# Decoder layer with a delta-rule scan, attention and experts: inverting by blocks of 32 rows and two rounds of doubling

## The chip, the cores and the metric

The kernel runs on one core of a Trainium2 chip. The metric is the device time of one execution in microseconds; a comparison of two kernels goes by the medians of their runs. The profile is one execution, recorded by the hardware.

## The reference

The input `x` is 32 sequences of 112 tokens with 256 features. One layer adds three blocks to it, each behind a layer norm: a recurrent block (an exponential average of the values, a delta-rule scan, a gated MLP), an attention with 16 heads over 375 context tokens, and a mixture of six experts of which each token takes two, with one shared expert. What the change touches is the scan:

```python
def step(S, inp):
    q_t, k_t, v_t, b_t = inp
    Sk = jnp.einsum('bij,bj->bi', S, k_t)
    S = S + b_t[:, None, None] * (v_t - Sk)[:, :, None] * k_t[:, None, :]
    o_t = jnp.einsum('bij,bj->bi', S, q_t)
    return (S, o_t)
```

Over 112 steps this is a triangular system. With G the products of the keys of one sequence, scaled by beta and the keys' norms, the kernel inverts a unit lower triangular matrix of 112 by 112 for each sequence and multiplies the values by the inverse.

## The kernel before

The 32 sequences go in eight groups of four (`GB`). For each group the stream `delta_block` followed by `queries` (together `ahead(g)`) does the recurrent block and the queries of the attention. The attention of a group takes 16 steps, each four heads of one sequence: `scores` (products, then the mask and the row extreme on VectorE, the exponential on ScalarE), two steps later `turned` (transposes, copied back by ScalarE) and `product`. Keys and values of the next sequence come from `keys_values`. While the attention of group g runs, the recurrent block of group g + 1 runs beside it, with the experts' routing and the shared expert of group g - 1 (`mixture_sparse`). In the last group the tables of the tokens for each expert are built (`tables`), and after it the experts run over them (`sparse_tiles`).

The order is made when the program is built. All instructions go to a `Recorder`. Streams are generators; each `yield` ends a piece, and the loop at the end of the kernel takes pieces in turn, by the matmul time that group 0's pieces cost (a piece with almost none counts 1.4 us). `Recorder.flush` then plans all engines with a price for each instruction (`price`) and emits them by planned start: whoever is ready first, and among the ready ones the earliest recorded. The order of TensorE, VectorE and ScalarE is taken as it is planned (`manual_schedule`); GpSimd and SyncE are ordered by the framework from the order in which it gets them. Every engine runs its instructions in order, so an instruction that comes later than its price said holds up what was planned behind its readers. The price of an operation on GpSimd with n elements per partition, a line of `price`, is

```python
return 0.97 if "dma" in op else 0.1 + n / 430
```

`hold()` makes the last recorded instruction follow the last recorded one of TensorE in the plan; it adds no wait on the chip.

The inversion in `delta_block`: the matrix W goes to a table in memory (`blocks<-W`), so that its diagonal blocks of 16 rows can be read back with one block on each partition (L, `C<-blocks`). A forward substitution inverts all 28 blocks at once, 15 steps of two operations, a product `part` and a subtraction. It runs on VectorE in group 0 and on GpSimd in the others (`plain`). The inverse and its transpose go back to two tables, which were cleared when the kernel began, and come back as block diagonal matrices X and Y of all four sequences (`X<-blocks`, `Y<-blocks`). Then rounds of doubling join neighbouring blocks, from 16 to 32, 64 and 112 rows: C (G between the halves, made on GpSimd) times X, scaled to W, then Y times W, subtracted from X (the last round updates Y instead). From the second round on Y is X turned by TensorE. All names in the profile are those of the buffers: the substitution appears as `W<-C,W` and `W<-W` with 28 partitions, a round as `X,C`, `W,Y` and `ident,X`. Most lines of the profile are L381, where the recorder emits.

In the routing, `dispatch` casts the places of the tokens in the experts' lists to integers (`row_i`) and scatters the tokens' numbers there with eight indirect DMAs of GpSimd, two for each sequence (the first and the second expert).

Of the kernel before, what the change touches and what calls it, by code (L numbers as in the profile page):

```python
# [8 lines left out]
F32 = mybir.dt.float32  # L9
# [3 lines left out]
ALU = mybir.AluOpType  # L13
# [3 lines left out]
P = 128  # L17
GB = 4
BS = 16
NEG = -1.0e9  # L20
# [365 lines left out]
def tile_decoder(ctx: ExitStack, tc: tile.TileContext, t: dict, out: bass.AP):  # L386
# [5 lines left out]
    nc = tc.nc  # L392
# [42 lines left out]

    NB = GB * T // BS
    FAR = BS * T + BS
    blocks = [dram.tile([NB, FAR], F32, name=f"blocks_{i}") for i in range(3)]
    kept = [dram.tile([GB, T, D], F32, name=f"kept_{g}") for g in range(groups - 1)]
# [12 lines left out]
    levels = []  # L452
    s = BS
    while s < T:
# [29 lines left out]
    nothing = moe.at("hT", 0, [P, t["fc3T"].shape[0] // P, NT])  # L484
    nothing = nothing[:T].rearrange("p c n -> p (c n)")[:, : NB * FAR // T]
    nc.vector.memset(nothing, 0.0)

    unit = const.tile([NB, BS, BS], F32, tag="unit", name="unit")
    nc.gpsimd.memset(unit, 0.0)
    nc.gpsimd.affine_select(  # L490
        out=unit, in_=unit, pattern=[[1, BS], [-1, BS]], compare_op=ALU.not_equal, fill=1.0, base=0,
        channel_multiplier=0,
    )
    number = const.tile([T, 2, SB], F32, tag="number", name="number")
# [21 lines left out]
    for vx in vxs:  # L516
        nc.gpsimd.memset(vx[:, :, :, 1, :], 0.0)
    for table in blocks[1:]:
        nc.gpsimd.dma_start(
            out=table.rearrange("n f -> (n f)").rearrange("(p q) -> p q", p=T), in_=nothing  # L520
        )
    for table in lists:
# [73 lines left out]
    keys_first, mask_first = load_keys(0), load_mask(0)  # L596
    xwk, xwv = weight("xwkT"), weight("xwvT")
    n2 = per_feature("norm2_w")
    wo = weight("Wo")
    w_gate, w_up, w_down = weight("w_gate"), weight("w_up"), weight("w_down")  # L600
    xwq, xwo = weight("xwqT"), weight("xwoT")
    keys_second, mask_second = load_keys(1), load_mask(1)
    x_second = load_x(1)
    gb = const.tile([T, NE], F32, tag="gb", name="gb")
# [94 lines left out]
    def delta_block(g, xt):  # L699
# [81 lines left out]
        plain.tensor_tensor(W, G, bcast(br2, T), ALU.mult)  # L781
        low, inv, turned_inv = blocks
# [3 lines left out]
        diagonal = lambda m: m[:, : BS * T].rearrange("n (i t) -> n i t", t=T)[:, :, :BS]  # L786
        nc.sync.dma_start(out=square(low), in_=W)
        L = dlt.tile([NB, BS, BS], F32, tag="C", name=f"L_{g}", bufs=2)
        nc.sync.dma_start(out=L, in_=diagonal(low))
        yield  # L790
        R = dlt.tile([NB, BS * BS + (BS // 2) ** 2], F32, tag="W", name=f"R_{g}", bufs=2)
        inverse = R[:, : BS * BS].rearrange("p (i j) -> p i j", j=BS)
        plain.tensor_copy(inverse, unit)
        for j in range(BS - 1):
            shape = [NB, BS - 1 - j, j + 1]
            part = R[:, BS * BS : BS * BS + shape[1] * shape[2]].rearrange("p (i j) -> p i j", j=j + 1)
            to = inverse[:, j + 1 :, : j + 1]
            plain.tensor_tensor(
                part, L[:, j + 1 :, j : j + 1].to_broadcast(shape),
                inverse[:, j : j + 1, : j + 1].to_broadcast(shape), ALU.mult,  # L800
            )
            plain.tensor_tensor(to, to, part, ALU.subtract)
            if j in (4, 9):
                yield
# [5 lines left out]
        nc.sync.dma_start(out=X, in_=square(inv))  # L810
        nc.sync.dma_start(out=Y, in_=square(turned_inv))
        yield
        yield
# [7 lines left out]

        C = between_halves(0)
        for i in range(len(levels)):
            pw = bank("pw")
# [3 lines left out]
            nc.vector.tensor_tensor(W, pw[:T, :NT].rearrange("p (b t) -> p b t", b=GB), bcast(br2, T), ALU.mult)  # L828
            if i > 0:
                py = bank("py")  # L830
                for b in range(GB):
                    transpose(py[:T, b * T : (b + 1) * T], X[:, b, :], ident[:T, :T])
                Y = dlt.tile([T, GB, T], F32, tag="Y", name=f"Y_{g}_{i}")
                nc.scalar.copy(Y.rearrange("p b t -> p (b t)"), py[:T, :NT])
# [269 lines left out]
    def dispatch(g, a3, place, ge):  # L1104
# [332 lines left out]
    def drain(stream):  # L1437
        for _ in stream:
            pass
# [196 lines left out]
```

## Time and profile before

| | |
|---|---|
| median of 13 runs | 1426.28 us (1423.45 to 1433.17) |
| profiled execution | 1423.26 us |
| its span, first to last instruction | 1421.6 us |
| granted TensorE clock, mean | 0.981 |
| busy TensorE, VectorE, ScalarE, GpSimd | 1362.6, 954.0, 702.6, 318.9 us |
| substitution of one group on GpSimd | 30 instructions, 409.07 to 419.52 us in group 3 |
| first matmul of a round in group 3 | 423.86 us |

Busy time is the union of an engine's instructions. The slices of the page are a fortieth of the span each, 35.5 us. PE is TensorE, DVE is VectorE, ACT is ScalarE, POOL is GpSimd, SP is SyncE, whose queue issues nearly all loads. A wait is put down to the engine or DMA that came last. A matmul of 32-bit floats has two records in the trace, a transpose one.

### The profile page before, as it was taken

What the parts mean: (1) busy time and instruction counts of PE and PEld (TensorE: products, weight loads), DVE (VectorE), ACT (ScalarE), POOL (GpSimd) and SP (SyncE); (2) the same over time, 40 slices, a digit from 0 to 9 for tenths busy, and PEclk for the clock granted to TensorE, in tenths of its full rate; (3) what the DMA queues carried; (4) which work ended last, traced back from release to release, by engine and by line L of the source; (5) the groups of instructions that cost most, each with busy time, mean ns of one, the idle gap of its engine ahead of it and who ended that gap; (6) DMA issues with size and microseconds to landing.
All of it is one profiled execution on the core that took longest, in us unless ns stands there. A gap on an engine that the chain in (4) does not pass through costs nothing.

```text
span 1421.6 us, 26678 instructions
## 1 busy us (share of the span) xinstructions
PE 1362.6 (96%) x9716; PEld 926.1 (65%) x9716; DVE 954.0 (67%) x3164; ACT 702.6 (49%) x1946; POOL 318.9 (22%) x492
## 2 busy tenths in 40 slices
PE   6679999999999899999999999999999999999998
PEld 4456766676677566766676667666766676666665
DVE  6646666775787487758775877587756875455577
ACT  2112856654665366456655664566556673222110
POOL 3122000311041103120312031203120045566400
PEclk9779999999999999999999999999999999999999
DMA  7100100101010100110011001100115122222283
GB/s 226 38 8 13 35 17 17 46 20 42 17 49 18 34 26 19 47 32 27 19 47 41 18 20 46 40 19 20 46 30 163 30 44 75 87 87 86 68 237 104
DMA packets 77170, 73.13 MB, mean 51 GB/s; under 512 B 29864, under 2 KB 72808, under 8 KB 77040
## 3 DMA queue, kind: packets, MB, share of 16 engines
q1 hardware_dynamic: 69296, 56.00, 14.5%
q0 software_dynamic: 7744, 15.43, 3.7%
q8 instruction: 77, 1.26, 0.4%
q14 instruction: 53, 0.43, 0.1%
HBM read 51.12 MB, written 20.28 MB: 50 GB/s over the span
## 4 chain that ended last, share of the span: by engine, by line
PE 71%; DVE 9%; ACT 6%; POOL 4%; DMA 4%; issue 2%; another core or an unknown queue 1%; SPq 0%; DVEq 0%; ACTq 0%
PE bank L381 61%; PE bank L1335 7%; PE bank L1352 3%; POOL W L381 3%; ACT e L381 3%; ACT eT L381 2%; DMA blocks<-W 2%; DMA X<-blocks 1%; DVE e L381 1%; DVE x L381 1%; DVE W L381 1%; DVE rs_u L381 1%; DVE rs_i L381 1%; ACT h L381 1%; DMA C<-blocks 1%
## 5 line engine op out<-in xcount | busy, mean ns | idle before, releaser
L381 ACT ACTIVATE e<-e,nmx 112x375 f32<-112x375 f32 x512 | 306.4, 603 | 176.0 <-DVE nmx L381 175.7
L381 DVE CUSTOM_DVE_ANT_0 e<-bank,neg,flip 112x375 f32<-112x375 f32 x512 | 282.7, 603 | 36.6 <-PE bank L381 30.9
L381 ACT COPY eT<-bank 125x448 f32<-125x448 f32 x384 | 185.3, 530 | 91.1 <-PE bank L381 81.7
L381 PEld LDWEIGHTS bank<-ident,e 112*125 112x125 f32 x1536 | 185.7, 188 | 31.3 <-issue 9.9
L381 PE MATMUL bank<-ident,e 112*125 112x112 f32 x1536 | 201.4, 276 | 1.0 <-ACT e L381 0.7
L381 PE MATMUL bank<-kx,qz 32*112 32x375 f32 x1024 | 123.4, 521 | 0.0
L381 PEld LDWEIGHTS bank<-eT,vx 125*32 125x32 f32 x3072 | 69.2, 109 | 57.2 <-issue 40.5
L381 PE MATMUL bank<-eT,vx 125*32 125x112 f32 x3072 | 100.7, 263 | 5.1 <-ACT eT L381 5.1
L381 PE MATMUL bank<-w_xwvT,cT 128*125 128x256 f32 x384 | 102.7, 394 | 0.0
L1335 PE MATMUL bank<-ew,xT 128*128 x216 | 101.9, 595 | 0.4 <-DVE nmx L381 0.4
L381 DVE SCALAR_TENSOR_TENSOR hs<-hs,bank 128x256 f32<-128x256 f32 x108 | 45.4, 421 | 79.5 <-ACT hs L381 77.6
L381 ACT ACTIVATION_READ_ACCUMULATOR e<-e,nmx 112x1 f32 x512 | 98.1, 192 | 0.0
L381 PE MATMUL bank<-cT,w_xwkT 128*128 128x375 f32 x256 | 95.4, 498 | 2.5 <-ACT eT L381 2.5
L381 POOL TENSOR_TENSOR u<-h,nwb 112x1024 f32<-112x1024 f32 x7 | 16.9, 2416 | 296.4 <-issue 282.8
L381 ACT ACTIVATE hs<-bank 128x256 f32<-128x256 f32 x54 | 20.7, 384 | 118.0 <-PE bank L1335 112.4
L381 POOL DMA_INDIRECT lists<-number,row_i x56 | 52.7, 941 | 110.5 <-DVE tn L381 57.0
L381 PEld LDWEIGHTS bank<-w_xwvT,cT 128*125 128x125 f32 x384 | 67.9, 190 | 13.7 <-issue 5.7
L381 DVE SCALAR_TENSOR_TENSOR qk<-qk,bank 128x448 f32<-128x448 f32 x56 | 34.8, 621 | 62.6 <-ACT qk L381 55.3
L381 PEld LDWEIGHTS bank<-cT,w_xwkT 128*128 128x128 f32 x256 | 44.0, 190 | 38.2 <-issue 6.9
L381 PEld LDWEIGHTS bank<-kx,qz 32*112 32x112 f32 x1024 | 42.2, 170 | 39.9 <-issue 15.6
L381 POOL DMA_INDIRECT xg<-rows,take x54 | 52.4, 969 | 51.6 <-PE bank L381 48.5
L1363 POOL DMA_INDIRECT results<-y,put x54 | 53.1, 983 | 38.5 <-DVE y L381 33.6
(251 smaller groups left out, 2380.0 us busy)
## 6 DMA issues: line engine op xcount, KB each, us to landing
cT<-in_ctxT_dram SPq DMA_DIRECT2D x32, 375.0 KB
mk<-in_mask_dram SPq DMA_DIRECT2D x32, 164.1 KB
x<-in_x_dram SPq DMA_DIRECT2D x7, 448.0 KB
rows<-h SPq DMA_DIRECT2D x7, 448.0 KB
kept<-x SPq DMA_DIRECT2D x7, 448.0 KB
e<-results SPq DMA_DIRECT2D x6, 448.0 KB
eT<-results SPq DMA_DIRECT2D x4, 448.0 KB
out_dram<-x SPq DMA_DIRECT2D x4, 448.0 KB
```

The source lines that it names most:

```text
L381: getattr(getattr(self.nc, name), op)(*[real(a) for a in args], **{k: real(v) for k, v in kwargs.items()})
L1335: rec.nc.tensor.matmul(p.real(), xT[:, c, :], w13[:, bass.ds(at[i] * (NC * 2 * MI) + c * 2 * MI, 2 * MI)], start=(c == 0), stop=(c == NC - 1),
L1352: rec.nc.tensor.matmul(p[:, :D].real(), hT[:, c, :], w2[:, bass.ds(at[i] * (CH * D) + c * D, D)], start=(c == 0), stop=(c == CH - 1),)
L1363: sent = rec.nc.gpsimd.indirect_dma_start(out=results[:], out_offset=bass.IndirectOffsetOnAxis(ap=put[:, i : i + 1], axis=0), in_=y, in_of ...
```

## The change

Group 0 keeps blocks of 16 rows and three rounds. In the other groups the blocks have 32 rows (four for each sequence, the last reaching past row 112 into cleared memory), so 16 partitions hold all blocks, the substitution has 31 steps with up to 256 elements, and two rounds follow. There are three more tables for it, cleared by SyncE during group 0. The unit matrix is set by two memsets in place of a copy; L, the inverse and `part` lie in other buffers in these groups. The substitution yields four times in place of twice, and two pauses stand in these groups where group 0 has its first round; the places of the keys' pieces in group 0 are moved to match. The places are cast for each sequence by itself, held behind TensorE, and the scatters of a sequence follow their cast. The loads of the second sequence's keys and mask and of the second group's tokens come before seven weights.

```diff
-BS = 16
+SIZES = 16, 32
...
+    many = [GB * ((T + size - 1) // size) for size in SIZES]
+    blocks = [
+        [dram.tile([n, size * T + size], F32, name=f"blocks_{size}_{i}") for i in range(3)]
+        for n, size in zip(many, SIZES)
+    ]
...
+    keys_second, mask_second = load_keys(1), load_mask(1)
+    x_second = load_x(1)
     n2 = per_feature("norm2_w")
     wo = weight("Wo")
     w_gate, w_up, w_down = weight("w_gate"), weight("w_up"), weight("w_down")
     xwq, xwo = weight("xwqT"), weight("xwoT")
-    keys_second, mask_second = load_keys(1), load_mask(1)
-    x_second = load_x(1)
...
-        L = dlt.tile([NB, BS, BS], F32, tag="C", name=f"L_{g}", bufs=2)
+        if g == 0:
+            L = dlt.tile([n, size, size], F32, tag="C", name=f"L_{g}", bufs=2)
+            spare = dlt.tile([n, size * size + (size // 2) ** 2], F32, tag="W", name=f"R_{g}", bufs=2)
+            flat, spare = spare[:, : size * size], spare[:, size * size :]
+        else:
+
+            L = qk.rearrange("p c n -> p (c n)")[:n, : size * size].rearrange("p (i j) -> p i j", j=size)
+            flat = dlt.tile([n, size * size], F32, tag="u", name=f"R_{g}")
+            spare = dlt.tile([n, (size // 2) ** 2], F32, tag="vs", name=f"part_{g}")
         nc.sync.dma_start(out=L, in_=diagonal(low))
         yield
-        plain.tensor_copy(inverse, unit)
-        for j in range(BS - 1):
+        plain.memset(flat, 0.0)
+        plain.memset(flat[:, :: size + 1], 1.0)
+        for j in range(size - 1):
...
-            if j in (4, 9):
+            if (j + 1) % (size // 4) == size // 8:
                 yield
...
+        first = min(g, 1)
+        for _ in range(2 * first):
+            yield
         yield
         yield
...
-        C = between_halves(0)
-        for i in range(len(levels)):
+        C = between_halves(first)
+        for i in range(first, len(levels)):
...
-            if i > 0:
+            if i > first:
                 py = bank("py")
...
-        nc.vector.tensor_copy(row_i[:, :, two], row_f[:, :, two])
         for b in range(GB):
+            i = g * GB + b
+            nc.vector.tensor_copy(row_i[:, :, i : i + 1], row_f[:, :, i : i + 1])
+            rec.hold()
             for c in range(2):
-                i = g * GB + b
                 nc.gpsimd.indirect_dma_start(
...
-                rec.hold()
...
-        for _ in range({5: 2, 6: 2, 7: 2, 8: 2, 9: 1, 11: 1, 18: 2}.get(i, 0)):
+        for _ in range({5: 2, 6: 2, 7: 1, 8: 1, 9: 1, 10: 1, 11: 1, 13: 1, 20: 2}.get(i, 0)):
             next(early_kv, None)
...
+        if i == 12:
+            for table in blocks[1]:
+                cleared(table, nc.sync)
+                rec.hold()
```

More of the change, by code (lines that the diff above doesn't have):

```diff
@@ L434, in tile_decoder @@
     results = dram.tile([2 * SB * T + NTM * TM, D], F32, name="results")
-    NB = GB * T // BS
-    FAR = BS * T + BS
-    blocks = [dram.tile([NB, FAR], F32, name=f"blocks_{i}") for i in range(3)]
+    many = [GB * ((T + size - 1) // size) for size in SIZES]
[3 more added lines that the diff above has]
+    ]
     kept = [dram.tile([GB, T, D], F32, name=f"kept_{g}") for g in range(groups - 1)]
@@ L452, in tile_decoder @@
     levels = []
-    s = BS
+    s = SIZES[0]
     while s < T:
@@ L484, in tile_decoder, with cleared @@
     nothing = moe.at("hT", 0, [P, t["fc3T"].shape[0] // P, NT])
-    nothing = nothing[:T].rearrange("p c n -> p (c n)")[:, : NB * FAR // T]
+    nothing = nothing.rearrange("p c n -> p (c n)")
     nc.vector.memset(nothing, 0.0)
[L488 to L493, printed above, removed]
+    def cleared(table, queue):
+        n = table.shape[0] * table.shape[1]
+        p = next(p for p in range(P, 0, -1) if n % p == 0 and n // p <= nothing.shape[1])
+        flat = table.rearrange("n f -> (n f)").rearrange("(p q) -> p q", p=p)
+        queue.dma_start(out=flat, in_=nothing[:p, : n // p])
     number = const.tile([T, 2, SB], F32, tag="number", name="number")
@@ L517, in tile_decoder @@
         nc.gpsimd.memset(vx[:, :, :, 1, :], 0.0)
[L518 to L521, printed above, removed]
+    for table in blocks[0][1:]:
+        cleared(table, nc.gpsimd)
     for table in lists:
@@ L781, in delta_block @@
         plain.tensor_tensor(W, G, bcast(br2, T), ALU.mult)
-        low, inv, turned_inv = blocks
+        size, n = SIZES[min(g, 1)], many[min(g, 1)]
+        low, inv, turned_inv = blocks[min(g, 1)]
         square = lambda m: m.rearrange("(b k) f -> b (k f)", b=GB)[:, : T * T].rearrange(
@@ L785, in delta_block @@
         )
-        diagonal = lambda m: m[:, : BS * T].rearrange("n (i t) -> n i t", t=T)[:, :, :BS]
+        diagonal = lambda m: m[:, : size * T].rearrange("n (i t) -> n i t", t=T)[:, :, :size]
         nc.sync.dma_start(out=square(low), in_=W)
-        L = dlt.tile([NB, BS, BS], F32, tag="C", name=f"L_{g}", bufs=2)
+        if g == 0:
[6 more added lines that the diff above has]
+            spare = dlt.tile([n, (size // 2) ** 2], F32, tag="vs", name=f"part_{g}")
         nc.sync.dma_start(out=L, in_=diagonal(low))
         yield
-        R = dlt.tile([NB, BS * BS + (BS // 2) ** 2], F32, tag="W", name=f"R_{g}", bufs=2)
-        inverse = R[:, : BS * BS].rearrange("p (i j) -> p i j", j=BS)
-        plain.tensor_copy(inverse, unit)
-        for j in range(BS - 1):
-            shape = [NB, BS - 1 - j, j + 1]
-            part = R[:, BS * BS : BS * BS + shape[1] * shape[2]].rearrange("p (i j) -> p i j", j=j + 1)
+        inverse = flat.rearrange("p (i j) -> p i j", j=size)
+        plain.memset(flat, 0.0)
+        plain.memset(flat[:, :: size + 1], 1.0)
+        for j in range(size - 1):
+            shape = [n, size - 1 - j, j + 1]
+            part = spare[:, : shape[1] * shape[2]].rearrange("p (i j) -> p i j", j=j + 1)
             to = inverse[:, j + 1 :, : j + 1]
```

## The prediction

> **What bounds the kernel now.** I read the busy shares and slices of the page first, then stretches of one group, the waits, and the rows of TensorE and GpSimd around one substitution.
>
> ```profile
> PE 1362.6 (96%) x9716; PEld 926.1 (65%) x9716; DVE 954.0 (67%) x3164; ACT 702.6 (49%) x1946; POOL 318.9 (22%) x492
> ...
> PE   6679999999999899999999999999999999999998
> ```
>
> TensorE is full from slice 4 on; only the head (the first 140 us) has gaps. The stretches (columns: stretch, its length, busy of PE, weight loads, DVE, ACT, POOL, granted clock, DMA share):
>
> ```profile
> 57.50:80.00 22.50, 12.85 (x57) 11.15 (x58) 8.10 (x19) 1.70 (x3) 2.64 (x3) 0.54 0.10 20
> 121.00:135.00 14.00, 11.38 (x70) 8.82 (x71) 9.62 (x29) 1.70 (x3) 1.13 (x1) 0.88 0.01 1
> 404.00:424.00 20.00, 19.59 (x207) 13.91 (x206) 18.65 (x74) 16.94 (x51) 10.70 (x33) 1.00 0.23 56
> 598.00:740.00 142.00, 140.19 (x1118) 97.32 (x1117) 101.08 (x349) 82.89 (x232) 26.75 (x47) 1.00 0.12 31
> ```
>
> A steady group takes 142 us, 140.19 of them TensorE. So work taken from TensorE there is time, and so is any wait put on it. Its waits between 380 and 450 us:
>
> ```profile
> PE bank L381 <- DVE nT L381: 0.8, 1, 0.8
> PE bank L381 <- DMA X<-blocks: 0.4, 1, 0.4
> ```
>
> The second is the end of the substitution's trip through memory. The trip on GpSimd, then the rounds of doubling on TensorE:
>
> ```profile
> 403.84 0.93 POOL L381 TENSOR_TENSOR W<-G,br 112x448 f32<-112x448 f32 x1
> 409.07 0.21 POOL L381 TENSOR_TENSOR W<-C,W 28x15 f32<-28x15 f32 x1 [4.30 <-DMA C<-blocks]
> 409.36 0.22 POOL L381 TENSOR_TENSOR W<-W 28x15 f32<-28x15 f32 x1
> ...
> 413.85 0.30 POOL L381 TENSOR_TENSOR W<-C,W 28x64 f32<-28x64 f32 x1
> 414.22 0.31 POOL L381 TENSOR_TENSOR W<-W 28x64 f32<-28x64 f32 x1
> 414.61 0.30 POOL L381 TENSOR_TENSOR W<-C,W 28x63 f32<-28x63 f32 x1
> ...
> 419.31 0.21 POOL L381 TENSOR_TENSOR W<-W 28x15 f32<-28x15 f32 x1
> ```
>
> ```profile
> 423.86 1.01 PE L381 MATMUL bank<-X,C 112*112 112x112 f32 x8 [0.41 <-DMA X<-blocks]
> 424.71 1.65 PE L381 MATMUL bank<-w_gate_wT,nT 128*112 128x6 f32 x16
> 426.21 1.02 PE L381 MATMUL bank<-W,Y 112*112 112x112 f32 x8
> 427.07 1.03 PE L381 MATMUL bank<-w_xwoT,oTx 128*112 128x256 f32 x4
> ...
> 429.58 0.55 PE L381 MATMUL bank<-ident,X 112*112 112x112 f32 x4
> 429.97 1.04 PE L381 MATMUL bank<-ident,vo 128*112 128x128 f32 x8
> ```
>
> The order on TensorE is fixed when the program is built. X came 0.41 us after TensorE turned to it: the order puts other work over the trip, by its prices.
>
> **The round that goes.** One round is eight records X,C, eight W,Y and four turns of X. From start to next start they hold TensorE 424.71-423.86 = 0.85, 427.07-426.21 = 0.86 and 429.97-429.58 = 0.39: 2.1 us. Groups 2 to 7 run this in full stretches: 6 x 2.1 = 12.6 us less. Group 1 stands under the head.
>
> **The longer substitution.** A block of 16 takes 15 pairs of instructions and 2 x 680 elements per partition; one of 32 takes 31 pairs and 2 x 5,456. Start to start is 0.29 us at 15 elements and 0.38 (mean of 0.37 and 0.39) at 64: 0.262 us each and 1.84 ns an element. That gives 30 x 0.262 + 1,360 x 0.00184 = 10.4 us for now (measured 419.52-409.07 = 10.45) and 62 x 0.262 + 10,912 x 0.00184 = 36.3 us after. Up to 256 elements are not in the trace; the rows of 448 bound them: W (932 ns) gives 1.63 ns beyond 64, hence 34.0 us, C (1134 ns) 2.16 ns, hence 39.8. I keep 36.3, the slope of the same instruction.
>
> GpSimd has the room (26.75 of 142 us busy). What counts is when X comes against the order's price, 0.1 + n/430 a piece: 6.2 us now and 6.2 + 25.4 = 31.6 after. The overrun is 10.45-6.2 = 4.3 now, with a wait of 0.4, and 36.3-31.6 = 4.7 after. The wait grows by 0.4 us a group, 2.4 in six; at 34.0 it vanishes (-2.4), at 39.8 it grows by 3.9, or 23.
>
> "GPSIMD Engine Reference", Engine selection and the accounting before it, speaks against this change: elementwise work belongs on VectorE, and a two-input operation costs GpSimd 4497 ns at 2048 elements. As an estimate from that page, 2.2 ns an element makes 40.2 us and the sum below some 23 us worse. The rows up to 64 elements say 1.84 ns, and the sum stays on them.
>
> **What covers it.** X comes 25.9 us later after W. TensorE must live that long on attention, keys and values. In 404 to 424 it did, idle only for X; but DVE was busy 18.65 of 20 us and ACT 16.94. Part of DVE's load there is a layer norm that comes once a group. I take 0.5 us of new idleness a group, 3 in six; ends 0 and a tenth of the stretch, 2.6, or 16. The same later X leaves fewer microseconds for the rest of the chain; before, xwq of this group ran at 522, 98 us after X, so 72 remain for work that group 0, alone, did in 63 (second round at 67.9, xwq at 131.2), and I charge nothing; without that cover it is the second rival.
>
> The copy that turns the inverse grows from 256 to 1,024 elements (0.60 to at most 2.4 us), so Y comes 1.8 us later against X. Y had 1.6 us to spare (issued 0.7 behind X, read 2.35 behind). The order prices the copy at 2.5 and plans around it: nothing, at worst 0.2 a group.
>
> On SP the stores of the inverse wait 26 us longer; behind them stood `rows<-h` and a mask load. The order is worked out anew and puts loads that are ready ahead of them: nothing, or, if a keys load lands behind, the second rival. The two memsets (1,024 elements, about 2.4 us by the u row) fall into GpSimd's 19.8 idle us before C.
>
> **The head.** Group 0 substitutes on VectorE as before. Its read of L was issued at 38.69 us and such a read takes 1.8 (407.25 to 409.07), yet VectorE began at 50.44: group 1's norm stood before it, and x of group 1 kept that waiting till 37.7. Its load moves from issue 20.2 to about 11. I take 4 us earlier (0 to 9.9). Against it: between 121.1 and 131.2 TensorE filled a gap with 4.8 us of group 1's rounds. They now come after a substitution 26 us longer; 2.1 are gone, 2.7 move into full stretches. The gap also lowers the clock (8 records took 1.81 us at 0.54, 0.85 at 1.00): 1 us, 0 to 3. Sum -4 + 2.7 + 1 = -0.3; ends -7.2 and +5.7.
>
> "TensorE: Matmul & The Clock Gate", Part 1, puts the fall of the clock after about 3.4 us without work. By it the waits for X above cost no clock; the 0.54 above is the case of this trace.
>
> **The rest.** Weights that now load later (Wo read at 86.9, w_gate at 100.7) have over 50 us. Clearing three tables by SP near 70 us falls where DMA is 0.10 busy; without that cover 3 x 226 KB at the 226 GB/s of the first slice cost 3 us. Three more casts a group, at 0.17 us, lie on VectorE at 67%. The eight scatters ran in one row (458.7 to 468.3), whatever the order said; now each pair waits for its cast. On GpSimd the gathers of the lists queue behind. In the last group scatters ended at 1144.5 and TensorE read the lists at 1164.1; the last cast should come after the shared products at 1150, and 3 us of scatters and 4 of gathers leave it about covered: 0.5 us, 0 to 3.
>
> **Sum.** -12.6 + 2.4 + 3 - 0.3 + 0.5 = -7.0 us. The profiled execution took 1423.26 (span 1421.6), so 1416.3; the median of the runs stands 3.0 above it, so 1419.3.
>
> **Rivals.** *Overrun, slower:* X is the new bound of each group. At 38.6 us of substitution, the wait grows by 2.7 instead of 0.4, +13.8: 1433; at 39.8, 1440. It decides from 37.5 us on (1.2 us more in six groups eats the 7.0), only 3% above my value. For it: rows of 448 elements at 2.16 ns; against it: the fit meets the 10.45. *Starved, slower:* TensorE idles 2.6 us a group over the long trip, +12.6: 1432. For it DVE's 93%; against it the unbroken 19.59. *Better, faster:* 34.0 us, no starving and the full head: -12.6 - 2.4 + 0.5 - 7.2 = -21.7: 1404.6. *Cancelled:* gains and waits meet, 1426. That a round is not saved I can exclude: the loop starts one level later.
>
> **Chances.** Measurement tells 0.2%, 2.9 us, from no change. Forecast 0.42 (own range 1410 to 1423.4), better 0.09, cancelled 0.14, overrun 0.22, starved 0.13. Faster 0.51, same 0.14, slower 0.35. The range 1408 to 1437 leaves out some 0.07 below and 0.12 above.
>
> **What would show it.** X,C, W,Y and turns of X fall to 136, 72 and 36 records; the substitution takes 34 to 40 us on GpSimd; the wait for X is about 0.8 us a group; a group takes some 140 us; VectorE starts group 0's substitution near 46. I am wrong if X's wait is over 2.5 us, if TensorE waits for ACT or DVE within the trip, or if the head ends later than 134.

## The result, and the profile after

The changed kernel takes 1495.19 us (median of 8 runs, 1490.09 to 1500.36) where the kernel before takes 1426.71 (median of 37): 1.0479 times as long, interval 1.0465 to 1.0493. The prediction said 1419.3, range 1408 to 1437. The profiled execution has a span of 1490.3 us against 1421.6, 68.7 more, and a mean granted clock of 0.955 against 0.981.

The busy shares and slices of the page of the changed kernel:

```profile
PE 1385.3 (93%) x9576; PEld 934.8 (63%) x9576; DVE 985.4 (66%) x3172; ACT 701.9 (47%) x1939; POOL 493.2 (33%) x714
...
PE   6687999999998999899989998999899998999998
...
PEclk9778999999999999899999998999899998999999
```

TensorE has 140 records fewer and yet 22.7 us more busy time. Its idle time rose from 1421.6 - 1362.6 = 59.0 to 1490.3 - 1385.3 = 105.0, by 46.0. The two rises are the 68.7. The slices show where: an 8 about once in every group, where before there was one in all groups together.

The waits of TensorE in one group (386.7 to 537 us) of the changed kernel:

```profile
PE bank L381 <- DMA X<-blocks: 5.5, 1, 5.5
PE bank L381 <- ACT eT L381: 0.7, 1, 0.7
PE bank L381 <- DVE taken L381: 0.5, 1, 0.5
PE bank L381 <- DVE flip L381: 0.4, 1, 0.4
PE bank L381 <- DVE h L381: 0.4, 1, 0.4
```

X, which came 0.4 us late before, comes 5.5 late. In the whole run the waits for X are 38.9 us (before: 8.0). How it gets there, on GpSimd, on SyncE's queue and on TensorE:

```profile
423.64 0.24 POOL L381 TENSOR_TENSOR vs<-qk,u 16x31 f32<-16x31 f32 x1 [5.10 <-DMA qk<-blocks]
...
460.29 0.24 POOL L381 TENSOR_TENSOR u<-u,vs 16x31 f32<-16x31 f32 x1
460.59 1.97 POOL L381 COPY qk<-u 16x1024 f32<-16x1024 f32 x1
462.74 0.99 POOL L381 DMA_INDIRECT lists<-number,row_i  x1 [0.17 <-DVE hT L381]
464.03 0.93 POOL L381 DMA_INDIRECT lists<-number,row_i  x1 [0.30 <-issue]
```

```profile
460.56 0.30 SPq L381 DMA_DIRECT2D blocks<-u  x1
462.59 0.30 SPq L381 DMA_DIRECT2D blocks<-qk  x1
462.94 0.48 SPq L381 DMA_DIRECT2D cT<-in_ctxT_dram  x1
463.48 0.59 SPq L381 DMA_DIRECT2D X<-blocks  x1
```

```profile
471.43 1.81 PE L381 MATMUL bank<-X,C 112*112 112x112 f32 x8 [5.54 <-DMA X<-blocks]
```

The substitution takes 460.53 - 423.64 = 36.9 us. From its end to X on TensorE it takes 10.9 us, where it took 423.86 - 419.52 = 4.3 before. Two things stand there that did not: on SyncE a load of keys (`cT`) between the stores of the inverse and X, and on GpSimd two scatters of places. Both queues work in order: what became ready on GpSimd during the substitution runs right behind it, and what SyncE got after the store of the inverse goes right behind that store, which waited for the substitution.

The stretch on both sides of X's wait, by windows (columns: stretch, its length, busy of PE, weight loads, DVE, ACT, POOL, clock, DMA share, GB/s):

```profile
463.50:466.00 2.50, 2.39 (x36) 1.76 (x34) 0.73 (x2) 1.41 (x3) 1.16 (x2) 1.00 0.83 222
466.00:471.40 5.40, 0.00 (x0) 0.00 (x0) 0.00 (x0) 0.00 (x0) 0.00 (x0) 0.72 1.19 61
...
471.00:474.50 3.50, 3.07 (x16) 2.03 (x16) 0.63 (x1) 0.00 (x0) 0.00 (x0) 0.50 0.31 42
```

All five engines stand still for 5.4 us. The DMA engines are marked busier than just before (1.19 against 0.83), but move 61 GB/s in place of 222. Behind the wait the clock is 0.50. (The last line is from a second table of the same view.)

### The profile page after: what moved, and what is told of

The parts are those of the page before. It is cut to its first block, busy times and chain, and to the rows that moved or that the text cites. A ratio compares the mean times of both kernels' runs of the same rounds, so it can differ in the third digit from the quotient of the medians.

```text
span 1490.3 us, 26678 instructions
## 1 busy us (share of the span) xinstructions
PE 1385.3 (93%) x9576; PEld 934.8 (63%) x9576; DVE 985.4 (66%) x3172; ACT 701.9 (47%) x1939; POOL 493.2 (33%) x714
## 5 line engine op out<-in xcount | busy, mean ns | idle before, releaser
L381 PE MATMUL bank<-kx,qz 32*112 32x375 f32 x1024 | 130.6, 552 | 0.0
L381 POOL TENSOR_TENSOR vs<-qk,u 16x31 f32<-16x31 f32 (+15 forms) x217 | 109.9, 506 | 51.8 <-DMA qk<-blocks 35.3
L381 POOL TENSOR_TENSOR u<-u,vs 16x31 f32<-16x31 f32 (+15 forms) x217 | 115.4, 532 | 17.0
L381 POOL TENSOR_TENSOR C<-G,ident 112x448 f32<-112x448 f32 x7 | 8.0, 1138 | 280.5 <-ACT G L381 280.5
L381 PE MATMUL bank<-ident,h 112*128 112x112 f32 x256 | 42.0, 284 | 30.7 <-ACT h L381 19.3
L381 PEld LDWEIGHTS bank<-cT,w_xwkT 128*128 128x128 f32 x256 | 44.2, 190 | 36.9 <-ACT eT L381 8.5
L381 POOL DMA_INDIRECT xg<-rows,take x54 | 52.7, 976 | 42.9 <-PE bank L381 40.2
## 6 DMA issues: line engine op xcount, KB each, us to landing
cT<-in_ctxT_dram SPq DMA_DIRECT2D x32, 375.0 KB, 3.8
```

Source lines behind the costliest of these rows:

```text
L381: getattr(getattr(self.nc, name), op)(*[real(a) for a in args], **{k: real(v) for k, v in kwargs.items()})
```

## The experiments

The runs came from several chips, and the kernel before took 1425 us on some and 1451 to 1459 on others; the changed kernel took 1495.2 at first and 1498.0 on a chip where the kernel before took 1451.3. So ratios are compared only between runs beside each other; they are all to the kernel before on the same chip. On the chip of places_back, pairs_loads, stores_pool and price the changed kernel itself was not run; nearest to a measure for them is its ratio on another chip with a slow kernel before, 1.0320 (after_again). In the changed kernel X's wait is 3.0 to 6.2 us in groups 2 to 7, 5.2 in the mean, and 7.5 in group 0, whose substitution is that of before; the waits given per group below are such means and leave group 0 out.

### The parts of the change

**places_back** undoes the pairs: one cast of all places, scatters with `hold` as before.

> The changed kernel with the places cast once and scattered as before. Theory that the pairs cost the end of the run: the eight scatters of the last group run in one row again, TensorE finds the lists without a wait, its share of the last stretch loses no clock, and the time falls by about 10 us, to 1485. Rival, that the end is late for another reason (the clock, or the group before it): within 2 us of 1495.

Measured: 1.0347 (1.0302 to 1.0392), 1508.9 us, on the chip of pairs_loads, stores_pool and price. The last stretch did not shorten: from the last queries on it took 354.5 us, where the changed kernel takes 343.7 and 346.5 on two other chips. Neither expectation holds. What the row did in the groups is seen from the waits: the eight scatters now ran in one row behind the substitution (469.0 to 478.7 in group 3), and X's waits are 37.6 us in six, group 0's among them.

**pairs_loads** is the kernel before with the two small edits.

> The kernel before (blocks of 16 rows, three rounds in every group) with the two small edits alone: the places in pairs and the second loads ahead. Theory that the pairs cost about 10 us and the loads ahead bring a few or nothing: 1433 to 1438. Rival, that the pairs only hurt beside the long substitution: 1423 to 1428. In both the blocks of 32 rows by themselves carry the rest, 57 to 72 us.

Measured: 1.0047 (1.0027 to 1.0067), 1464.7 us against 1458.6. So the blocks carry most of the loss. The pairs seem to cost something even with short blocks: the last stretch took 347.2 us (333.6 in the kernel before, but on other chips), and the next group's tokens landed late, here beside scatters at 350.4 and 351.7:

```profile
346.26 0.33 SPq L381 DMA_DIRECT2D x<-in_x_dram  x1
```

```profile
358.86 0.43 DVE L381 BATCH_NORM_STATS2 bst<-x 112x6 f32<-112x256 f32 x1 [8.72 <-DMA x<-in_x_dram]
```

That is 12.6 us for a load whose median in the changed kernel is 3.8. It was the first sign that the scatters, and not the keys load, are what makes a load late.

**loads_only** is the kernel before with the loads ahead alone (run later, when the sum for the head had failed).

> The kernel before with the second keys, mask and tokens loaded ahead of the seven weights, and nothing else. By the head of the changed kernel, where the queries of group 0 stood 1.4 us earlier although TensorE lost its filling, and of the kernel with this and the pairs, 1.3 us earlier: 1 to 3 us less, 0.998 to 0.9995 times the kernel before. If the later weights hold something up: 1.001 or more.

Measured: 0.9969 (0.9954 to 0.9984), 1419.8 us against 1425.6. It is faster than both kernels. Its first scores:

```profile
117.20 0.95 PE L381 MATMUL bank<-X,C 112*112 112x112 f32 x8
...
125.89 3.19 PE L381 MATMUL bank<-nT,w_xwqT 128*128 128x448 f32 x8
129.01 1.21 PE L381 MATMUL bank<-kx,qz 32*112 32x375 f32 x11
```

They start at 129.0 where they started at 134.3. The gain of the loads ahead is there when group 1's rounds stand in the gap before the queries. In the changed kernel that gap is empty:

```profile
126.52 0.45 PE L381 MATMUL bank<-ident,h 112*128 112x112 f32 x1 [6.85 <-DVE h L381]
...
129.79 5.30 PE L381 MATMUL bank<-nT,w_xwqT 128*128 128x448 f32 x8
135.02 1.21 PE L381 MATMUL bank<-kx,qz 32*112 32x375 f32 x11
```

The same eight matmuls of the queries take 5.30 us in place of 3.19, and the scores start 0.7 us later than before.

### Why X is late

**stores_pool** issues the inverse's stores on GpSimd's own queue.

```diff
-        nc.sync.dma_start(out=diagonal(inv), in_=inverse)
-        nc.sync.dma_start(out=diagonal(turned_inv), in_=L)
+        queue = nc.gpsimd if g else nc.sync
+        queue.dma_start(out=diagonal(inv), in_=inverse)
+        queue.dma_start(out=diagonal(turned_inv), in_=L)
```

> The changed kernel with the two stores of the inverse issued by GpSimd's own queue in groups 1 to 7, so that SyncE is not held by them and the keys load behind them goes ahead. Theory that this load between the stores and X makes X late: the way from the end of the substitution to X falls from 10.9 us to about 5, X's wait from 5.5 to about 1 us a group, and with it most of the half clock after it; 30 to 50 us less, 1445 to 1465. Rival, that the overrun of the price (36.9 us against 31.6) makes X late: X's wait stays at 4 to 6 us and the time within 10 us of 1495. Rival, that the clock is lost to small gaps in the stretch over the substitution: X's wait falls, but the clock there stays at 0.5 to 0.8 and no more than 25 us come back.

Measured: 1.0419 (1.036 to 1.0478). The keys load went ahead as meant (452.22), but X's load, with no keys load near, issued at 471.38 and still came to TensorE at 479.34: 8.0 us. The scatters stood at 470.1 and 471.4. From the end of the substitution (466.37) to X it took 13.0 us, not about 5. X's wait fell to (26.6 - 7.0) / 6 = 3.3 us a group only because TensorE came to X later. So the keys load alone does not make X late; what share it has, this run does not tell.

**price** plans with the measured price.

```diff
-            return 0.97 if "dma" in op else 0.1 + n / 430
+            return 0.97 if "dma" in op else 0.262 + n / 543
```

> The changed kernel with the price of GpSimd's operations as measured, 0.262 us and 1.84 ns an element, which plans X 4.8 us later. Theory of the overrun: X's wait falls under 1 us and 30 to 45 us come back. Theory of the load behind the stores: the wait falls only if the new plan also puts the keys load ahead of the stores; where it still stands between them and X, the way from the substitution to X stays near 11 us, the wait at 1 to 2 us a group, and 25 to 35 us come back. Theory of the small gaps: the wait falls and the clock of the stretch over the substitution stays under 0.8; under 25 us come back.

Measured: 1.0312 (1.0253 to 1.0371), the best of these four but for pairs_loads, and not to be told from the 1.0320 of the changed kernel on another chip, where 25 to 45 us were expected back. X's wait went in four of the six groups, and others came in its place: TensorE waited 12.5 us for `u`, 11.3 for `nmx` and 6.2 for Y. X's load in group 3 was as slow as before, issued at 467.88 and read at 475.47; the plan only came to it later. So mending the overrun of the price by itself moved the wait and brought nothing that can be told: the late load was still late for whoever came next.

After these four the scatters were the theory, and the next four ran side by side. **after_again** is the changed kernel itself.

> The changed kernel unaltered, as the measure for the runs beside it on the same chip. Expected: 1.045 to 1.052 times the kernel before, X's wait 5 to 6 us a group.

Measured: 1.0320 (1.0284 to 1.0356), 1498.0 us; X's wait 5.5 us a group (3.2 to 7.6). The ratio is under the 1.045 expected because the kernel before is slower on this chip.

**scatters_end** records the scatters of groups 0 to 5 at the start of the last group.

> The changed kernel with the 48 scatters of the places of groups 0 to 5 taken out of their groups and issued at the start of the last group; the casts stay, and the order on SyncE is the same, with the keys load between the stores of the inverse and X. Theory of the scatters: GpSimd runs them right behind the long substitution, where X is loaded, and while they write, every load beside them goes several times slower (packets of 448 bytes took 25 ns before them and 60 to 330 ns behind them); without them X lands within 4 us of its issue, its wait falls from 5.5 to at most 1.5 us in groups 2 to 7, and 30 to 45 us come back there; the last group may lose up to 20, its tables waiting for 60 us of scatters. Theory of the keys load that stands ahead of X: X lands as late as before, wait 5 to 6 us, and the groups stay as long as they are.

Measured: 1.0308 (1.0279 to 1.0336), nothing changed. The experiment did not do what it says: the framework orders GpSimd itself, took the scatters as ready after their casts, and put them where they had been (467.8 and 469.1 in group 3). To move them, the cast must move, since VectorE's order is the plan's. It serves as a second run of the changed kernel.

**short_keys** was to cut the keys load ahead of X; it leaves out a quarter of the keys.

```diff
-        nc.sync.dma_start(out=cT, in_=ctxT[b].rearrange("(c p) k -> p c k", p=P))
+        some = slice(0, 4 if b >= 4 and b % 4 == 3 else SK)
+        nc.sync.dma_start(out=cT[:, :, some], in_=ctxT[b].rearrange("(c p) k -> p c k", p=P)[:, :, some])
```

> The changed kernel with the keys load that stands between the inverse's stores and X (the last sequence of each group) cut from 375 to 4 columns, so that a quarter of the keys of the context is left out. Theory of the keys load: X lands within 4 us, its wait falls under 1.5 us, 30 to 45 us come back. Theory of the scatters: X still lands 6 us or more behind its issue and the wait stays at 4 to 6 us; under 12 us come back.

Measured: 1.0364 (1.0333 to 1.0396), no better; X's wait (43.8 - 6.9) / 6 = 6.1 us a group. In group 3 X's load, issued at 468.40, came at 474.44, scatters at 467.5 and 468.8. But the edit missed its load. It cuts the keys of each group's last sequence, and the load ahead of X is for the next group's first. The DMA views around the two loads, issued at 417.25 and at 467.70:

```profile
cT<-in_ctxT_dram SPq DMA_DIRECT2D x1, 4.0 KB
```

```profile
cT<-in_ctxT_dram SPq DMA_DIRECT2D x1, 375.0 KB
```

So the whole keys load still stood right ahead of X, and this run says nothing of it.

**pairs_later** moves the first casts behind X.

```diff
-            if i < GB:
-                first()
+            for _ in range(2 if later else 1):
+                if later <= i < GB:
+                    first()
```

> The changed kernel with the cast and scatter of the first two sequences of groups 0 to 5 put two pieces of the shared expert later, so that the first pair's cast comes some 20 us later, behind X's load. Theory of the scatters: X lands within 4 us and its wait falls under 1.5 us; the slow stretch moves to the loads that come next (keys, the next group's tokens), and 20 to 40 us come back. Theory of the keys load: wait 5 to 6 us as before, under 5 us come back. If the cast still comes before X in the order, nothing changes and the run tells nothing apart.

Measured: 1.0289 (1.0254 to 1.0323). In group 3 the substitution's end was followed by nothing on GpSimd until

```profile
495.02 1.00 POOL L381 DMA_INDIRECT lists<-number,row_i  x1 [27.22 <-DVE row_i L381]
```

and X's load, issued at 468.71 with the keys load right ahead of it, was on TensorE at 473.50. That stretch by windows:

```profile
468.70:473.50 4.80, 1.85 (x32) 1.25 (x30) 0.42 (x1) 0.88 (x3) 0.00 (x0) 1.00 0.89 210
```

210 GB/s at a DMA share of 0.89, against 61 at 1.19 with the scatters. X's median landing, from the DMA views of the changed kernel and of this one (the last column is us from issue to landing):

```profile
X<-blocks SPq DMA_DIRECT2D x8, 196.0 KB, 7.6
```

```profile
X<-blocks SPq DMA_DIRECT2D x8, 196.0 KB, 4.5
```

The page can tell the landing of only some of these loads; from issue to TensorE's read, with TensorE waiting each time, X took 6.9 to 9.0 us in groups 2 to 7 of after_again, on the same chip, and 4.4 to 5.3 here. X's wait fell to (26.1 - 7.3) / 6 = 3.1 us. But only 3 us of the whole came back, since the scatters met other loads. In the group from 238 us on, VectorE's first read of the next group's tokens stood for them, and TensorE behind it:

```profile
357.90 2.87 PE L381 MATMUL bank<-cT,w_xwkT 128*128 128x375 f32 x4 [7.03 <-DVE nmx L381]
```

### Taking the scatters out of the way

**quiet** casts a group's places at once, at step 14 of the 16 of the attention beside it; group 6's as before the change.

```diff
+        if i == 14 and 0 < g < groups - 1:
+            cast_and_scatter(g - 1)
```

> The changed kernel with the places of groups 0 to 5 cast at once, near the end of each group (step 14 of 16, behind the loads), and the eight scatters in a row behind that cast; group 6 casts and scatters at once as the kernel before does. Theory of the scatters: no load has a scatter beside it, X lands within 5 us of its issue, X's wait falls from 5.5 to 2 or 3 us (the overrun of the price, the copy ahead and the keys load remain), no other load is slow, and of the end some 7 us come back: 25 to 40 us less than the changed kernel, 1.01 to 1.025 times the kernel before. Rival, that the clock is lost to the small gaps whatever X does: under 15 us.

Measured: 1.0655 (1.0617 to 1.0694), 1547.7 us, the slowest of all, and the expectation missed by 57 us from its slow end. X behaved as the theory says: its wait is 17.9 / 6 = 3.0 us. But step 14 was not quiet here. One row ran from 528.4 to 538.1, and the next keys load, issued at 540.68, moved at 32 GB/s:

```profile
540.70:553.20 12.50, 8.75 (x56) 6.37 (x57) 4.57 (x16) 5.45 (x16) 0.00 (x0) 0.74 0.70 32
```

From 236 to 1187 TensorE waited 17.5 us for nothing that the profile shows and 5.5 for values (`vx`). So a row of eight with a load behind it did more harm here than the pairs.

**quiet_keys** is the same with the edit of short_keys.

> The kernel with the quiet scatters and the keys load ahead of X cut from 375 to 4 columns (a quarter of the keys left out). Of the way from the substitution to X, 10.9 us against 4.35 before, the scatters by the runs so far account for some 3.4 and the copy of the turned inverse for 1.3; the keys load should account for the rest, 1.9: X lands 2.5 to 3 us behind its issue, and its wait is 1.5 to 2.5 us below that of the kernel with the quiet scatters alone. If the keys load costs nothing, X lands as late in both.

Measured: 1.0593 (1.0553 to 1.0633). X's wait is (23.9 - 7.5) / 6 = 2.7 us, 0.3 below quiet, not 1.5 to 2.5. But the load ahead of X is whole here too (375.0 KB, issued at 467.52, X at 468.78), so the 0.3 is not its price.

**quiet_short** leaves the substitution at 10 of 31 steps.

> The kernel with the quiet scatters, its substitution in groups 1 to 7 cut to the first 10 of 31 steps, which by the measured rates take 10.3 us, as blocks of 16 do; the inverse is left unfinished. What remains of the change is the round that goes. Theory that the length of the way is the whole loss: the groups fall to 139 or 140 us, X's wait under 1 us, and the time 5 to 13 us below the kernel before. Rival, that something else of the change costs (the memsets, the copy, the new order): above the kernel before.

Measured: 1.0234 (1.0205 to 1.0263), between both. X's wait was gone, so its lateness is that of the long way. But from 218 to 1115 TensorE waited 13.3 us for `qz` and 5.1 for `mk` (a copy in the masks' buffer), both written by VectorE. Why VectorE is behind in this order was not followed up, and the run does not give the round's gain by itself. It does show X's load with neither a keys load ahead nor scatters near, behind stores of the same 64 KB:

```profile
882.84 0.30 SPq L381 DMA_DIRECT2D blocks<-qk  x1
883.25 0.43 SPq L381 DMA_DIRECT2D X<-blocks  x1
```

```profile
886.25 0.95 PE L381 MATMUL bank<-X,C 112*112 112x112 f32 x8
```

X was there within 3.0 us, as in the kernel before (2.7 in group 3). In quiet, with the keys load ahead and no scatters near, it took 4.2 to 5.5.

**quiet_price** joins quiet and price. The plan that the price makes puts the rows elsewhere.

> The kernel with the quiet scatters and the measured price of GpSimd's operations (0.262 us and 1.84 ns an element). Theory that X's lateness is the bulk of the loss: X's wait is under 0.5 us, no load behind it is late, the time comes within 10 us of the kernel before, on either side. Rival, that the long stretch without the group's own work starves TensorE: X's wait is gone, but small gaps and half clocks over the substitution remain, and the time stays 15 to 30 us above the kernel before.

Measured: 0.9992 (0.9972 to 1.0012), 1453.4 us against 1454.2: 94 us less than quiet on the same chip, and level with the kernel before there. No load is late in it:

```profile
cT<-in_ctxT_dram SPq DMA_DIRECT2D x32, 375.0 KB, 3.2
...
X<-blocks SPq DMA_DIRECT2D x8, 196.0 KB, 4.3
```

In group 3 X's load was issued at 458.63 and X read without a wait at 464.10. X waits in group 0 alone.

### What remains when X is in time

**before_again** is the kernel before on the chip of the next two.

> The kernel before, unaltered, for its profile on the chip of the runs beside it, so that groups and the last stretch can be laid side by side. Expected: groups of 141 to 145 us, the stretch from the last queries on 334 to 340 us, X's wait under 0.7 us, no load slow beside scatters.

Measured: 1420.7 us, span 1419.0, its groups 139.9 to 140.9 us from 523 on, the last stretch 333.6.

**quiet_pairs** is quiet_price with the pairs in group 6.

> The kernel with the quiet scatters and the measured price, but with the places of group 6 in pairs, as the changed kernel has them. Without them its last stretch took 356 us with 10.7 us of waits for nothing that the profile shows, all beside the row of eight scatters; the changed kernel with pairs took 344 to 348. Theory that the row of scatters costs the end here: the last stretch falls to 344 to 348 us and the time to 1440 to 1446 on the same chip, 0.99 to 0.995 times the kernel before. Rival, that the end is long for another reason (the clock): 0.998 to 1.002, as with the row.

Measured: 1.0132 (1.0112 to 1.0152), 1443.1 against 1424.9. The last stretch is 344.4 us as expected, but the ratio is not, since the kernel before is faster on this chip. The group from 804.6 in before_again and from 814.2 in quiet_pairs:

```profile
804.60:945.50 140.90, 139.15 (x1110) 96.44 (x1110) 100.70 (x349) 82.40 (x229) 26.80 (x47) 1.00 0.12 32
```

```profile
814.20:955.20 141.00, 137.06 (x1089) 94.86 (x1088) 104.00 (x347) 81.21 (x227) 51.92 (x79) 1.00 0.12 32
```

TensorE works 2.09 us less, the round that goes (2.1 predicted). It idles 3.94 in place of 1.75 us, 2.19 more. The group is as long as it was. Its waits:

```profile
PE bank L381 <- DVE qk L381: 1.1, 1, 1.1
PE bank L381 <- DVE taken L381: 1.0, 1, 1.0
PE bank L381 <- ACT eT L381: 0.7, 1, 0.7
PE bank L381 <- DVE flip L381: 0.4, 1, 0.4
PE bank L381 <- DVE h L381: 0.3, 1, 0.3
PE bank L381 <- ACT e L381: 0.2, 1, 0.2
```

All are VectorE and ScalarE. `taken`, `eT`, `flip` and `h` fall into the long substitution (846.8 to 883.8), during which TensorE idles 2.5 us; in before_again it idles not at all during the short one (839.9 to 850.2). `qk` comes behind it. The rest of this kernel's loss is the last stretch (344.4 - 333.6 = 10.8) and the beginning: up to the queries of group 2 it took 387.1 us, before_again 374.8.

**before_price** is the kernel before with the measured price alone.

> The kernel before with the measured price of GpSimd's operations and nothing else: what the price alone is worth where blocks have 16 rows. X there waits 0.4 us a group, 2.5 in six. If the price helps only by X's wait: 0.997 to 1.000 times the kernel before. Rival, that the price, and not the blocks, brings the kernel with the quiet scatters down to the kernel before: 0.99 or less.

Measured: 1.0024 (1.0011 to 1.0036), a little slower. The price is not what brought quiet_price down; it is worth something only where the substitution is long.

**late32** keeps blocks of 16 in group 1 too.

```diff
-        size, n = SIZES[min(g, 1)], many[min(g, 1)]
+        first = 1 if g > 1 else 0
+        size, n = SIZES[first], many[first]
```

> The kernel with quiet scatters, measured price and the pairs of group 6, with blocks of 16 rows and three rounds in group 1 too, so that only groups 2 to 7 have blocks of 32. On one chip the stretch up to the queries of group 3 (head and the attention of groups 0 and 1) took 374.8 us in the kernel before and 387.1 with blocks of 32 from group 1 on, where group 1's rounds no longer fill the head's last gap. Theory that this is the loss at the beginning: the stretch falls to 375 to 379 us and the time by 8 to 12 us, to 1.005 to 1.008 times the kernel before. Rival, that the loads ahead or the tables' clearing cost it: at most 3 us back, 1.011 or more.

Measured: 1.0084 (1.0058 to 1.011). The beginning (up to the queries of group 2; the expectation miscounts them as group 3's) took 379.1 us, 8.0 less than in quiet_pairs on another chip, as expected. loads_only, on the same chip, has that mark at 369.8, so some loss stays there, but by the last queries the two are level, 1083.2 and 1084.1 us. What still divides them is the last stretch, 344.9 against 333.6.

**late32_row** is late32 with the places of group 6 cast at once.

> The kernel with blocks of 32 from group 2 on, quiet scatters and measured price, and the places of group 6 cast at once, their eight scatters in a row as in the kernel before. With pairs there its groups ended (mark of the last queries) at 1083.2 us and the last stretch took 344.9; the kernel before took 333.6 for that stretch with the row, two kernels with long blocks and the row took 354 to 356, with waits for nothing that the profile shows. If the row's cost depends on where it falls, and falls well here: 333 to 337 us, 0.993 to 0.998 times the kernel before, and the blocks of 32 are worth a little once all is mended. If the row starves TensorE again: 352 to 358 us, 1.012 to 1.018.

Measured: 1.0011 (0.9998 to 1.0023). Its last group before the end and its last stretch:

```profile
802.70:944.80 142.10, 138.58 (x1090) 95.80 (x1089) 104.46 (x347) 81.34 (x227) 51.90 (x79) 0.99 0.13 32
...
1083.70:1421.00 337.30, 328.43 (x1847) 211.14 (x1846) 209.00 (x622) 113.79 (x324) 121.19 (x124) 0.99 0.34 96
```

The group is 142.1 us long, against 140.9 in before_again. The row cost little this time (337.3 us against 354.5 and 356.4), but not by where it fell: in this stretch the order of quiet_price is the same, instruction for instruction, on every engine. What differs is the chip (see the last section) and, far ahead of it, group 1. All that the runs had named is mended but the small gaps. What comes out is the time of the kernel before, no less, with the loads ahead, which brought 0.3% by themselves, already in it. So the blocks of 32 rows gave nothing in any form that was run.

## Why the prediction was wrong, point by point

| term | predicted, us | measured in the profile, us |
|---|---|---|
| work of a round gone | -12.6 (groups 2 to 7) | 7 x -2.09 (from quiet_pairs) = -14.6 |
| waits for X | +2.4 | 38.9 - 8.0 = +30.9 |
| other idle time of TensorE | +3 in groups | (105.0 - 38.9) - (59.0 - 8.0) = +15.1, of which 6.8 in the last stretch |
| TensorE's busy time but for the round | +1 (head) | 22.7 + 14.6 = +37.3 |
| sum | -7.0 with the small terms | +68.7 of span |

**The substitution** was sized right: 36.3 us predicted, 36.9 measured; GpSimd's operations of up to 256 elements follow the fit made at 15 and 64. (The ends of 34.0 and 39.8 us apply their slopes to all elements; beyond 64 alone, as the prediction says, they would be 34.8 and 38.6, which decides nothing.) The estimate of 40.2 us from "GPSIMD Engine Reference" was too high for this shape. The rival Overrun, which was to decide from 37.5 us on, did not decide.

**The way behind it is the step that failed.** The prediction took it as unchanged but for the overrun (a wait of 0.8 us, "on SP ... nothing"). It grew from 4.3 to 10.9 us. Of the 6.6, 1.3 lie before the issue: 463.48 - 460.53 = 2.95 against 421.19 - 419.52 = 1.67, since X's load stands on SyncE behind the store of the turned inverse, which waits for the copy of 1.97 us. The prediction let that copy delay Y, not X. The other 5.3 are the load itself, 7.95 us from issue to TensorE against 2.67. Taking the scatters away gives back 3.1 of it (medians 7.6 and 4.5). The remaining two go with the keys load right ahead of X: with neither near (quiet_short) X is there within 3.0 us, behind stores as large (64 KB, where the kernel before has 28). No run took the keys load away alone, so its share is argued from that row.

**The scatters** stood in the prediction, under "The rest", with a price for the last stretch alone. It was said there that each pair waits for its cast; it was not asked what GpSimd does with a pair that is ready while 62 operations stand ahead of it. It runs it right behind them, and that is the moment when X is loaded. Of SyncE the question was asked: "if a keys load lands behind" was named, given to the second rival and left out of the sum. The load did land there.

**The clock** was priced at 1 us in the head. By the mean clock, (1 - 0.955) x 1490.3 = 67 us of full speed were withheld, against (1 - 0.981) x 1421.6 = 27 before; the 40 between them are about the 37.3 of the table. Part of it is seen behind X's wait (0.50 above), part inside the substitution:

```profile
434.00:437.50 3.50, 3.03 (x46) 2.46 (x44) 2.24 (x7) 0.81 (x2) 3.11 (x6) 1.00 0.62 179
437.50:441.00 3.50, 3.50 (x15) 1.97 (x15) 2.81 (x10) 1.40 (x5) 3.11 (x6) 0.53 0.00 0
```

The clock falls behind a stretch in which TensorE idled 0.47 us of 3.5. "TensorE: Matmul & The Clock Gate", Part 1, ties the fall to about 3.4 us without work; the prediction quoted it as saying that waits for X below a microsecond cost no clock. The waits of 5.5 us that came agree with it, the fall at 437.5 does not. Nor does the kernel before, where the clock fell behind a wait for X of 0.36 us (at 572.0):

```profile
571.20:574.60 3.40, 3.04 (x46) 2.82 (x35) 2.82 (x9) 2.43 (x9) 1.13 (x1) 1.00 0.83 245
574.60:578.00 3.40, 3.40 (x14) 2.87 (x13) 2.19 (x9) 0.59 (x3) 0.00 (x0) 0.50 0.00 0
```

So the prediction's step from small waits to no loss of clock was wrong in this kernel already.

**The cover** over the long way was put at 0.5 us a group with 2.6 as its end; it is 2.2, near the end. So the rival Starved had the right mechanism for what is left when X is in time, and it takes the whole gain of the round. The row that the 0.5 came from, idle only for X in 20 us, was a stretch in which the rounds themselves were at hand.

**The head** was put at -0.3. X of group 0 did come 62.76 - 58.92 = 3.84 us earlier (4 predicted), but the gap that group 1's rounds had filled stood open, the queries took 5.30 us in place of 3.19, and those of group 1 came at 236.0 in place of 228.6: +7.4. The loads ahead alone gave their gain (0.9969).

**The last stretch** was put at +0.5, ends 0 and 3. It grew by 10.1 (343.7 against 333.6):

```profile
1233.16 1.26 PE L381 MATMUL bank<-ident,hs 54*128 54x54 f32 x3 [6.84 <-DMA hs<-lists,tsrci]
```

Each gather of the lists waits for the scatter just ahead of it, so the last list comes behind the last pair.

The prediction's own signs of being wrong all appeared: X's wait over 2.5 us, waits for ScalarE and VectorE within the way, and scores that start after 134.

## What to carry to other kernels

A long piece of work on an in-order engine moves everything that is queued behind it to its end: list what becomes ready meanwhile on that engine and on every queue that waits for it, because it will all run at the one moment when the result is on its way. Where the time of a plan is mended (a price, a place), run the mends together as well as alone: quiet alone took 1.0655 times the kernel before and price alone (on another chip) 1.0312, and both together 0.9992. And a saving on the bound engine is worth only what the other work can cover; here 2.1 us of matmuls a group were paid with a substitution 26 us longer, and TensorE lost 2.2 us a group to VectorE and ScalarE, most of it during that substitution. And see in the trace that an edit reached what it was meant for: two runs on the keys load and one on the scatters did not.

## What the runs showed of the hardware

- Loads beside or just behind small scatters (112 elements of 4 bytes each) slow down several times: X's load had 61 GB/s at a DMA share of 1.19 with two scatters near, 210 at 0.89 without. Moving the scatters moved the slow load with them, to the tokens, the keys or X. "DMA: Bandwidth & Descriptors", section "Issuing engines are not separate DMA queues", says that what GpSimd and SyncE issue runs on the same 16 engines and interleaves; these runs agree, and show that a small transfer beside a large one can slow it more than threefold. What inside the DMA engines does it, no run here shows.
- In quiet_price TensorE nearly stopped beside the row of scatters and the gathers of the last stretch, without a wait that the profile names, and ScalarE and VectorE with it:

```profile
1153.80:1166.50 12.70, 3.54 (x11) 1.23 (x11) 1.64 (x4) 0.00 (x0) 8.53 (x9) 0.55 0.31 19
```

Waits of this kind make 9.9 us of places_back's last stretch too, and none of late32_row's, whose order there is that of quiet_price. That engines lacked instructions, whose loading is DMA too (queue "instruction" on the page), is a guess.
- The kernel before differs by 2% between chips (1425 and 1451 to 1459 us), the changed one hardly (1495.2 and 1498.0). That is why no ratio here is carried from one set of runs to another. The last stretch tells where much of it may lie: with a row of eight scatters it takes 353.9 to 356.4 us in places_back, quiet, quiet_keys and quiet_price, all on chips where the kernel before is slow, and 333.6 to 337.3 in the kernel before, loads_only and late32_row on the others. With pairs it takes 345.4 to 348.6 and 343.7 to 344.9. So the row costs some 20 us more on those chips. That this is the 26 to 33 us that the kernel before loses there is not shown, since it was not profiled on one of them; and what makes those chips different is open.
